# First unit: queries ahead of the keys, more work on VectorE, stacks sent strip by strip, and the test of the square weights at the beginning

## The chip, the cores and the metric

The kernel runs on one core of one Trainium2 chip. The metric is the device time of one execution in microseconds, as the median of three runs. The five engines appear in the profile as PE (TensorE, matmuls; PEld is its loading of weights), DVE (VectorE), ACT (ScalarE), POOL (GpSimd) and SP (SyncE, which here does nothing but issue DMAs). SPq and ACTq are the DMAs that the SP and the ACT queue issue; while ACT issues a DMA it does nothing else.

## The reference

Eight sequences of 512 positions and 128 features go through six attention layers and then through a gated network. The attention is unusual: the softmax weights of 16 heads are averaged, a decay is added, and a second softmax of that sum is applied to `h` itself.

```python
def layer(h, p):
    q = (h @ wq.T + bq_).reshape(bh, sl, H, DH)      # H = 16, DH = 8
    k = (h @ wk.T + bk_).reshape(bh, sl, H, DH)
    scores = jnp.einsum('blhd,bmhd->bhlm', q, k) * inv_sqrt_d
    w_avg = jax.nn.softmax(scores, axis=-1).mean(axis=1)
    new_w = jax.nn.softmax(CSCALE * w_avg + rel[None], axis=-1)
    sa = jnp.einsum('blm,bme->ble', new_w, h)
    h1 = _ln(h + sa, l1w, l1b)
    h2 = _ln(h1, l2w, l2b)
    ff = jax.nn.relu(h2 @ w1.T + b1_) @ w2.T + b2_
    return (_ln(h2 + ff, l3w, l3b), None)

x = x + layers(_layernorm(x))                        # 6 layers, 8 sequences of (512, 128)
h = _layernorm(x)
h = jax.nn.silu((h @ w1.T) * s1) * ((h @ w2.T) * s2) # 128 -> 512
h = gelu((h @ h1.T) * sh1); h = gelu((h @ h2.T) * sh2)  # 512 -> 512, twice
return x + (h @ w3.T) * s3                           # 512 -> 128
```

`w1_w`, `w2_w`, `h1_w` and `h2_w` of the last network hold only -1, 0 and 1.

## The kernel before

**Units and steps.** The work is cut into 48 units, one for each layer and sequence (layer 0 with sequences 0 to 7, then layer 1, and so on). A unit has four blocks `lc` of 128 query positions, a block has four strips (`turn`) of four heads, and a strip is worked in two halves: 32 steps (`PAIRS`) to a unit. A step issues two matmuls of scores (L461, 128 x 512), two maxima of them on DVE (L472, `top`), and two exponentials on ACT (L481, `e`), so a unit has 64 of each. Every second strip the sums of the exponentials are inverted (L490, `r`), POOL makes from them weights `rp` (L492), and PE gathers the heads into one accumulator (L503, `acc`). After four strips ACT takes the second exponential (L511, `w`), PE transposes it, DVE multiplies it by the decay (L521) and PE applies it to `h` (L529).

**An order written by hand.** There is no scheduler. `at(step, place, fn)` files a piece of work under a step and a place in it (P0 to P2 between the matmuls, D0 to D2 between the maxima, A0 to A2 between the exponentials), and the main loop issues it there. So each engine's order is fixed by the program, and an instruction that waits holds up all that follow on its engine. `plan_before` files what a unit needs before its scores, `plan_after` its norms and its feed-forward part, which run in the two units behind. Steps below 0 are the start, before the first scores.

**Stacks.** A matmul of scores takes its keys from `ks` and its queries from `qs`, both laid out by strip. Keys and queries are split into a high part (12 low bits cleared, `hik`, `hiq`, on DVE, L283) and the rest (`lok`, `loq`, on POOL, L284). POOL multiplies the query parts by a mask of heads (L320, into tiles `m0` and `m1`), and DMAs inside the on-chip memory carry the pieces to their strips: 16 of 64 KB for the keys of a unit (`stack_k`, L299) and 16 of 128 KB for each half of its queries (`stack_q`, L336). For the first half of the first unit `stack_first` (L347) does it in 32 of 64 KB, 16 for each of the blocks 0 and 1. There the keys go first (steps 4 and 6 of the start), the queries after (steps 8, 18 and 19), and the ACT queue issues half of the key DMAs and half of those of block 0. The masked queries of block 1 lie in two of the four buffers of the tiles of exponentials (`e`), which thus come free when those DMAs have landed.

**Start.** SP loads two sequences and all weights of layer 0 (L98, L107 to L113), ACT nine small tables (L127). The first two norms run on DVE (statistics) and POOL (the power of -1/2, then subtract, L210, and multiply, L215). PE's clock is the granted clock of the profile.

**Ring and buffers.** The results of matmuls go to seven banks in a ring (`ps_big`), so PE can be some seven tiles ahead of ACT. The pool `proj` has two buffers each for `ks` and `qs`. DMAs are tracked by eight semaphores in turn, so each DMA issued on SP or ACT waits until the one eight before it has landed.

**Test of the square weights.** Whether the last network may use a cheaper exact product depends on the low 12 bits of the eight 128 x 512 blocks of `h1`, `h2` and of `w1`, `w2`. In the units 41 to 45 `load_square` (steps 1 and 16) brings two blocks each to a staging tile and from there to its place, and `low_bits` (steps 7 and 23) clears the high bits on DVE (L159) and takes the maximum (L162). In unit 47 `low_bits_row` and `low_bits_end` reduce this to one number, which after the last unit chooses an arm of the program.

Of the kernel before, what the change touches and what calls it, by code (L numbers as in the profile page):

```python
# [29 lines left out]
def attn_stack_then_ffn(ctx: ExitStack, tc: tile.TileContext, a: dict, out: bass.AP):  # L30
# [69 lines left out]

    for b in range(2):
        x_in[b] = load_x(b, f"in{b}")
    lay = {}

    def load_layer(d):
        qk = wts.tile([P, 2, E], F32, tag="wqk", name=f"wqk_{d}", bufs=2)
        nc.sync.dma_start(qk, a["wqk"][d].rearrange("t e o -> e t o"))  # L107
# [9 lines left out]
        rows = {name: r[:, k, :] for k, name in enumerate(ROWS)}  # L117
        lay[d] = (qk, w1, w2, rows)

    cols = {}  # L120
    for name, shape in (
        ("bq_col", [P, D]), ("bk_col", [P, D]), ("b1_col", [P, D * FC]),
        ("ln2w_col", [P, D]), ("ln2b_col", [P, D]), ("f_w1s_col", [P, HC]),
        ("f_w2s_col", [P, HC]), ("f_h1s_col", [P, HC]), ("f_h2s_col", [P, HC]),
    ):
        cols[name] = wts.tile(shape, F32, tag=name, name=name)
        nc.scalar.dma_start(cols[name], a[name])  # L127
    load_layer(0)

# [15 lines left out]
    staged = {}  # L145

    def load_square(k):

        name, c = ("f_w1t", "f_w2t", "f_h1t", "f_h2t")[k if k < 2 else 2 + (k - 2) // HC], (k - 2) % HC
        t = staged[k] = state.tile([P, HID], F32, tag="x", name=f"square_{k}", bufs=3)  # L150
        nc.sync.dma_start(t, a[name] if k < 2 else a[name][c * P : (c + 1) * P, :])
        nc.sync.dma_start(
            (fw1, fw2)[k] if k < 2 else (fh1, fh2)[(k - 2) // HC][:, c, :], t
        )

    def low_bits(k):

        t = staged.pop(k)
        nc.vector.tensor_scalar(  # L159
            t.bitcast(I32), t.bitcast(I32), ~LOW12, None, ALU.bitwise_and  # L160
        )
        nc.vector.tensor_reduce(low[:, k : k + 1], t.bitcast(I32), AX.X, ALU.max)  # L162

# [20 lines left out]
    class Norm:  # L184
# [57 lines left out]
    class Unit:  # L242
# [18 lines left out]
        def project_k(self):  # L261
            d = self.d
            pk = ring([P, L], f"pk_{self.n}")
            self.kT = work.tile([P, L], F32, tag="kT", name=f"kT_{self.n}", bufs=1)
            nc.tensor.matmul(pk, lay[d][0][:, 1, :], self.hT, start=True, stop=True)  # L265
            return lambda: nc.scalar.activation(  # L266
                self.kT, pk, AF.Identity, bias=cols["bk_col"][:, d : d + 1]
            )

        def project_q(self):  # L270
            d = self.d
            pq = ring([P, L], f"pq_{self.n}")
            self.qT = work.tile([P, L], F32, tag="qT", name=f"qT_{self.n}", bufs=1)
            nc.tensor.matmul(pq, lay[d][0][:, 0, :], self.hT, start=True, stop=True)
# [18 lines left out]
        def stack_k(self):  # L293


            self.ks = proj.tile([P, STRIPS, L], F32, tag="ks", name=f"ks_{self.n}")
            for c in range(4):
                for i in range(STRIPS):
                    (nc.scalar if self.u == 0 and c % 2 else nc.sync).dma_start(  # L299
                        self.ks[32 * c : 32 * c + 32, i, :],  # L300
                        self.kparts[c % 2][32 * i : 32 * i + 32, :],
                    )

        def mask_q(self, two, k, lc):
# [3 lines left out]
            if self.u == 0 and two == 0:  # L308
                pool, tag = (work, f"m{k}") if lc == 0 else (epool, "e")
                self.stacks[key] = pool.tile(  # L310
                    [P, 2, NB, PER_STRIP, QB], F32, tag=tag, name=f"m{k}_first_{lc}",
                    bufs=1 if lc == 0 else None,
                )
            elif lc == 2 * two:
# [25 lines left out]

        def stack_first(self, lc):

            if lc == 0:
                self.stacks[0] = proj.tile([P, STRIPS, 2, NB * P], F32, tag="qs", name="qs_first")
            for i in range(STRIPS):
                for c in range(4):
                    (nc.scalar if c >= 2 and lc == 0 else nc.sync).dma_start(  # L347
                        self.stacks[0][32 * c : 32 * c + 32, i, lc],
                        self.stacks[0, c // 2][32 * i : 32 * i + 32, lc].rearrange(
                            "p n j l -> p (n j l)"  # L350
                        ),
                    )


        def sum_rows(self):

            rows = lay[self.d][3]
            rows["b2s"] = wts.tile([P, E], F32, tag="b2s", name=f"b2s_{self.d}", bufs=2)
            nc.gpsimd.tensor_tensor(rows["b2s"], rows["ln2_b"], rows["b2"], ALU.add)
# [5 lines left out]
        def affine_a(self, k):  # L365
            rows = lay[self.d][3]
            if k == 0:
# [8 lines left out]
        def affine_b(self, k):  # L376
            rows = lay[self.d][3]
            if k == 0:
# [14 lines left out]
        def hidden(self, f):  # L393
            w1 = lay[self.d][1]
            if f == 0:
# [317 lines left out]
    def plan_before(un):  # L713
# [7 lines left out]
        s = t - PAIRS  # L721
        matmuls(s, (2, P2, 2, A1), un.project_k)
        matmuls(s, (6, P0, 7, A1), un.project_q)
        at(s + 4, D1, un.split_k)
        at(s + 8, D2, un.split_q)
        at(s + 6, D2, un.stack_k)
        for k in range(2):
# [3 lines left out]
        if un.b == 0:  # L731
            at(t + 3, D2, un.sum_rows)
        if un.u == 0:
            for lc in range(2):
                for k in range(2):
                    at(s + 18 + lc, D2, lambda k=k, lc=lc: un.mask_q(0, k, lc))
                at(s + 18 + lc, D2, lambda lc=lc: un.stack_first(lc))
            return
# [285 lines left out]
```

## Time and profile before

| what | value |
|---|---|
| median of 3 runs (lowest, highest) | 2611.12 us (2611.08, 2613.16) |
| the profiled execution's own time | 2611.54 us |
| span of its profile | 2609.7 us |
| busy: PE, DVE, ACT, POOL | 97%, 95%, 94%, 70% |
| first matmul of scores, first exponential | 28.53 us, 30.80 us |
| last exponential starts | 2389.2 us |
| DMA: moved, mean rate | 273.75 MB, 105 GB/s |

The three busiest engines are all close to full for the whole run, so no single one can be named from the shares alone. The first and the last tenth of the profile differ from the middle; the last 220 us are the gated network.

A useful clock of this kernel is the start of the first exponential of each unit, which the timeline shows (64 of them to a unit):

| from unit to unit | us for one unit |
|---|---|
| 0 to 1, 1 to 2 | 49.3, 48.8 |
| 2 to 5 | 49.8 to 49.9 |
| 6 to 40 | 48.9 to 49.1 |
| 41 to 45 | 50.3 each |
| 46 | 49.7 |

### The profile page before, as it was taken

How to read it: one execution, taken by the hardware profiler on the slowest of the kernel's cores; microseconds unless marked ns; L12 is line 12 of the kernel's file. 1: busy time of each engine (PE TensorE's matmuls, PEld its weight loads, DVE VectorE, ACT ScalarE, POOL GpSimd, SP SyncE). 2: the span in 40 equal slices, each digit the busy share in tenths (PEclk: the TensorE clock that was granted, in tenths of full speed). 3: DMA queues.
4: the chain of work that ended last, by engine and by line, in shares of the span. 5: the costliest groups of instructions: out<-in, count | busy, mean ns of one | idle time of the engine just before them, and what ended most of it. 6: DMA issues, size and time to landing. Idle time of an engine off the chain costs nothing.

```text
span 2609.7 us, 51735 instructions
## 1 busy us (share of the span) xinstructions
PE 2526.3 (97%) x14944; PEld 1435.9 (55%) x14944; DVE 2482.6 (95%) x5582; ACT 2450.8 (94%) x6798; POOL 1834.0 (70%) x1990
## 2 busy tenths in 40 slices
PE   5999999999999999999999999999999999998999
PEld 2455555555555555555555555555555555555787
DVE  5999999999999999999999999999999999998874
ACT  5999999999999999999999999999999999997443
POOL 4667777677677677677677677677677667775974
PEclk8999999999999999999999999999999999999999
DMA  5554544444444444444444444444444545541000
GB/s 133 116 120 119 116 112 100 114 114 115 114 114 98 114 110 119 114 114 98 114 113 115 114 109 103 114 113 116 114 113 104 138 117 128 132 102 34 9 25 18
DMA packets 135857, 273.75 MB, mean 105 GB/s; under 512 B 39696, under 2 KB 57232, under 8 KB 135568
## 3 DMA queue, kind: packets, MB, share of 16 engines
q1 hardware_dynamic: 133504, 269.31, 44.1%
q8 instruction: 121, 1.98, 0.3%
q10 hardware_dynamic: 2064, 1.08, 0.2%
q14 instruction: 168, 1.38, 0.2%
HBM read 13.86 MB, written 2.10 MB: 6 GB/s over the span
## 4 chain that ended last, share of the span: by engine, by line
PE 46%; ACT 33%; DVE 12%; issue 4%; POOL 3%; DMA 0%; ACTq 0%; SPq 0%; DVEq 0%; POOLq 0%
ACT e L481 28%; PE ps L461 14%; PE acc L503 13%; DVE top L472 9%; PE py L418 4%; PE qh L589 4%; PE po L529 3%; PE pt_w L222 2%; ACT w L511 2%; PE pf L398 1%; PE fo L635 1%; ACT kT L266 1%; PE q L589 1%; ACT g L406 1%; PE pk L265 1%
## 5 line engine op out<-in xcount | busy, mean ns | idle before, releaser
L481 ACT ACTIVATE e<-ps,top 128x512 f32<-128x512 f32 x3072 | 2137.7, 814 | 19.7 <-DMA qs_first<-m_first 9.3
L472 DVE TENSOR_REDUCE top<-ps 128x1 f32<-128x512 f32 x3072 | 1923.2, 677 | 24.5 <-PE ps L461 19.6
L461 PE MATMUL ps<-ks,qs 128*128 128x512 f32 x3040 | 1153.8, 468 | 16.0 <-ACT e L481 14.1
L481 ACT ACTIVATION_READ_ACCUMULATOR e<-ps,top 128x1 f32 x3072 | 1021.1, 332 | 0.0
L461 PEld LDWEIGHTS ps<-ks,qs 128*128 128x128 f32 x3040 | 524.1, 188 | 623.6 <-ACT e L481 322.4
L503 PE MATMUL acc<-e,rp 128*32 128x512 f32 x6144 | 739.1, 599 | 0.0
L503 PEld LDWEIGHTS acc<-e,rp 128*32 128x32 f32 x6144 | 160.3, 109 | 330.5 <-issue 328.8
L492 POOL TENSOR_TENSOR rp<-pick,r 128x256 f32<-128x256 f32 x384 | 237.2, 618 | 122.6 <-DVE r L490 77.6
L320 POOL TENSOR_TENSOR m<-loq,mask 128x512 f32<-128x512 f32 x190 | 241.6, 1283 | 0.0
L320 POOL TENSOR_TENSOR m<-hiq,mask 128x512 f32<-128x512 f32 x190 | 241.5, 1282 | 0.0
L529 PEld LDWEIGHTS po<-h,wT 128*128 128x128 f32 x1536 | 201.1, 191 | 20.5 <-issue 3.6
L529 PE MATMUL po<-h,wT 128*128 128x129 f32 x1536 | 203.5, 275 | 1.0 <-DVE wT L521 1.0
L284 POOL TENSOR_TENSOR loq<-qT,hiq 128x512 f32<-128x512 f32 x48 | 61.5, 1282 | 197.8 <-DVE hiq L283 173.5
L398 PE MATMUL pf<-uT,w 128*128 128x512 f32 x384 | 195.9, 591 | 0.9 <-ACT ht L625 0.9
L418 PEld LDWEIGHTS py<-w,g 128*128 128x128 f32 x1536 | 186.1, 191 | 8.4
L418 PE MATMUL py<-w,g 128*128 128x128 f32 x1536 | 186.8, 275 | 0.0
L222 PE MATMUL pt_w<-ident,w 128*128 128x128 f32 x768 | 120.6, 279 | 21.8 <-ACT e L481 13.3
L511 ACT ACTIVATE w<-acc 128x512 f32<-128x512 f32 x192 | 135.6, 706 | 1.1 <-PE acc L503 1.1
L521 DVE TENSOR_TENSOR wT<-pt_w,decay 128x512 f32<-128x512 f32 x192 | 130.3, 678 | 0.0
L222 PEld LDWEIGHTS pt_w<-ident,w 128*128 128x128 f32 x768 | 87.7, 140 | 74.6 <-ACT e L481 55.4
L206 POOL TENSOR_TENSOR rs_c<-mv_c,eps 128x4 f32<-128x4 f32 x48 | 9.7, 203 | 166.1 <-DVE mv_c L200 166.1
L406 ACT ACTIVATE g<-pf,b_col 128x512 f32<-128x512 f32 x144 | 125.3, 870 | 0.2 <-PE pf L398 0.2
(118 smaller groups left out, 2633.9 us busy)
## 6 DMA issues: line engine op xcount, KB each, us to landing
qs<-m SPq DMA_DIRECT2D x1520, 128.0 KB, 2.3
ks<-hik SPq DMA_DIRECT2D x384, 64.0 KB, 2.0
ks<-lok SPq DMA_DIRECT2D x376, 64.0 KB, 2.0
rows<-in_rows SPq DMA_DIRECT2D x6, 448.0 KB, 4.8
x_in<-in_x SPq DMA_DIRECT2D x8, 256.0 KB, 3.0
fh<-square SPq DMA_DIRECT2D x8, 256.0 KB, 2.3
x_out<-in_x SPq DMA_DIRECT2D x8, 256.0 KB, 2.8
out<-y SPq DMA_DIRECT2D x7, 256.0 KB, 2.4
```

Of the source, the lines that this page charges most:

```text
L222: nc.tensor.transpose(pt[:, c * P : (c + 1) * P], src[:, c, :], ident)
L320: nc.gpsimd.tensor_tensor(m[:, lc - 2 * two], part.unsqueeze(2).to_broadcast([P, NB, PER_STRIP, QB]), mask.unsqueeze(1).to_broadcast([P, N ...
L398: nc.tensor.matmul(pf, w1[:, f * P : (f + 1) * P], self.uT, start=True, stop=True)
L406: nc.scalar.activation(self.g[:, f, :], pf, AF.Relu, bias=cols["b1_col"][:, k : k + 1])
L418: nc.tensor.matmul(self.py[:, k, :], self.g[:, f, c * P : (c + 1) * P], w2[:, f, :], start=(f == 0), stop=(f == FC - 1),)
L461: nc.tensor.matmul(ps[s], qs[:, nb * P : (nb + 1) * P].bitcast(F32R), un.ks[:, i, :].bitcast(F32R), start=True, stop=True,)
L472: nc.vector.tensor_reduce(top[s], ps[s], AX.X, ALU.max, negate=True)
L481: nc.scalar.activation(self.e[:, nb, :], ps[s], AF.Exp, bias=top[s], accum_out=self.zs[:, i % 2, nb : nb + 1],)
L492: nc.gpsimd.tensor_tensor(self.rp.rearrange("p t n l -> p (t n) l"), pick.unsqueeze(1).to_broadcast([P, 2 * NB, QB]), r.rearrange("p t n - ...
L503: nc.tensor.matmul(acc[nb * QB : (nb + 1) * QB, :], self.rp[:, gr.turn % 2, nb, :], gr.e[:, nb, :], start=(gr.turn == 0), stop=(gr.turn == ...
L511: nc.scalar.activation(self.w.rearrange("p c l -> p (c l)"), acc, AF.Exp, scale=1.0 / H)
L529: nc.tensor.matmul(self.po, self.wT[:, c, :], self.unit.h[:, c, 0 : E + 1], start=(c == 0), stop=(c == LC - 1),)
```

## The change

The start and the first unit are put in another order, and the test of the square weights is moved from the units 41 to 47 to the start and the first unit.

- Loads: SP now issues first the first sequence, `wqk` of layer 0 and the tables `bq_col`, `bk_col`, then ten loads of 256 KB of the square weights for the test (`look_at_square`, into the first `ks` and `qs` buffers), then the second sequence and the seven other tables. ACT loads nothing. `w1`, `w2` and `rows` of layer 0 are loaded in unit 0, behind the first stacks.
- First two norms: subtract and multiply are one DVE instruction per 128 x 128 block (`centre_and_scale`) in place of two POOL instructions.
- First unit: the queries are projected and split before the keys, and `lo` is subtracted on DVE. POOL's masks for the blocks 0 and 1 follow at once; those of block 1 lie in a buffer of `g` and no longer in tiles of exponentials.
- `stack_first` sends keys and queries of block 0 strip by strip: for the strips 0 to 2, four DMAs on SP and four on ACT; for strip 3 all eight on SP. Then 16 for block 1 on SP. In all SP issues 36 and ACT 12 of these (32 and 16 before).
- `sum_rows` (POOL, 0.47 us) moves from step 3 to step 12 of unit 0.
- Test: `low_bits` works on two blocks at a time (128 x 1024) in five parts: parts 0, 1 and 2 before the first scores, parts 3 and 4 at the steps 4 and 6 of unit 0; the reduction to one number at its step 8 and at the first step of unit 1. `load_square` in the units 41 to 45 stays, with its DMAs; the ten DVE pairs there and the two instructions in unit 47 are gone.

```diff
+    x_in[0] = load_x(0, "in0")
+    load_qk(0)
+    load_col("bq_col", [P, D])
+    load_col("bk_col", [P, D])
...
-    low = state.tile([P, 2 + 2 * HC], I32, name="low")
+    low = state.tile([P, 1 + HC], I32, name="low")
...
+    def look_at_square():
+        first = proj.tile([P, 2, HID], F32, tag="ks", name="look_first")
+        rest = proj.tile([P, 2 * HC, HID], F32, tag="qs", name="look_rest")
+        for part in range(1 + HC):
+            looked[part] = first if part == 0 else rest[:, 2 * part - 2 : 2 * part, :]
+            for k in range(2):
+                nc.sync.dma_start(looked[part][:, k, :], square_block(2 * part + k)[0])
...
+    def low_bits(part):
+        t = looked.pop(part).bitcast(I32)
+        nc.vector.tensor_scalar(t, t, ~LOW12, None, ALU.bitwise_and)
+        nc.vector.tensor_reduce(low[:, part : part + 1], t, AX.XY, ALU.max)
...
+    look_at_square()
+    x_in[1] = load_x(1, "in1")
+    for name, shape in other_cols:
+        load_col(name, shape)
...
+        def centre_and_scale(self):
+            for c in range(LC):
+                nc.vector.tensor_scalar(
+                    self.dst[:, c, :], self.src[:, c, :], self.mv[:, c, 0:1], self.rs[:, c : c + 1],
+                    ALU.subtract, ALU.mult,
+                )
...
-            nc.gpsimd.tensor_tensor(lo, t, hi, ALU.subtract)
+            (nc.vector if self.u == 0 else nc.gpsimd).tensor_tensor(lo, t, hi, ALU.subtract)
...
-                pool, tag = (work, f"m{k}") if lc == 0 else (epool, "e")
...
+                        self.m_first = work.tile(
+                            [P, 2, 2, NB, PER_STRIP, QB], F32, tag="g", name="m_first", bufs=1
+                        )
...
+        def stack_first(self):
+            self.ks = proj.tile([P, STRIPS, L], F32, tag="ks", name="ks_first")
+            self.stacks[0] = proj.tile([P, STRIPS, 2, NB * P], F32, tag="qs", name="qs_first")
...
+            for i in range(STRIPS):
+                queries(nc.sync, i, 0, 0)
+                keys(nc.sync, i, 0)
+                other = nc.scalar if i < STRIPS - 1 else nc.sync
+                keys(other, i, 1)
+                queries(other, i, 0, 1)
+            for i in range(STRIPS):
+                for k in range(2):
+                    queries(nc.sync, i, 1, k)
...
+        if un.u == 0:
+            matmuls(s, (4, P0, 4, A0), un.project_q)
+            matmuls(s, (4, P1, 5, A0), un.project_k)
+            at(s + 5, D0, un.split_q)
+            for lc in range(2):
+                for k in range(2):
+                    at(s + (5, 6)[lc], D2, lambda k=k, lc=lc: un.mask_q(0, k, lc))
+            at(s + 6, D0, un.split_k)
+            at(s + 6, D2, un.stack_first)
...
-            at(t + 3, D2, un.sum_rows)
+            at(t + (12 if un.u == 0 else 3), D2, un.sum_rows)
...
+    for k, step in enumerate((-30, -30, -26, 4, 6)):
+        at(step, D2, lambda k=k: low_bits(k))
+    at(8, D2, low_bits_row)
+    at(PAIRS, D2, low_bits_end)
...
         at((U - 7 + k // 2) * PAIRS + (1, 16)[k % 2], D2, lambda k=k: load_square(k))
-        at((U - 7 + k // 2) * PAIRS + (7, 23)[k % 2], D2, lambda k=k: low_bits(k))
-    at((U - 1) * PAIRS + 7, D2, low_bits_row)
-    at((U - 1) * PAIRS + 23, D2, low_bits_end)
...
         if un.b == 4 and un.d + 1 < D:
+            load_qk(un.d + 1)
             load_layer(un.d + 1)
+        if u == 0:
+            load_layer(0)
```

More of the change, by code (lines that the diff above doesn't have):

```diff
@@ L99, in load_x, with load_qk @@
         return t
-    for b in range(2):
-        x_in[b] = load_x(b, f"in{b}")
-    lay = {}
+    lay_qk, lay = {}, {}
+    def load_qk(d):
+        lay_qk[d] = wts.tile([P, 2, E], F32, tag="wqk", name=f"wqk_{d}", bufs=2)
+        nc.sync.dma_start(lay_qk[d], a["wqk"][d].rearrange("t e o -> e t o"))
     def load_layer(d):
-        qk = wts.tile([P, 2, E], F32, tag="wqk", name=f"wqk_{d}", bufs=2)
-        nc.sync.dma_start(qk, a["wqk"][d].rearrange("t e o -> e t o"))
         w1 = wts.tile([P, F], F32, tag="w1", name=f"w1_{d}", bufs=2)
@@ L116, in load_layer, with load_col @@
         )
-        rows = {name: r[:, k, :] for k, name in enumerate(ROWS)}
-        lay[d] = (qk, w1, w2, rows)
+        lay[d] = w1, w2, {name: r[:, k, :] for k, name in enumerate(ROWS)}
+    x_in[0] = load_x(0, "in0")
+    load_qk(0)
     cols = {}
[L121 to L125, printed above, removed]
-        cols[name] = wts.tile(shape, F32, tag=name, name=name)
-        nc.scalar.dma_start(cols[name], a[name])
-    load_layer(0)
+    def load_col(name, shape):
+        cols[name] = wts.tile(shape, F32, tag=name, name=name)
+        nc.sync.dma_start(cols[name], a[name])
+    load_col("bq_col", [P, D])
+    load_col("bk_col", [P, D])
+    other_cols = (
+        ("b1_col", [P, D * FC]), ("ln2w_col", [P, D]), ("ln2b_col", [P, D]),
+        ("f_w1s_col", [P, HC]), ("f_w2s_col", [P, HC]), ("f_h1s_col", [P, HC]),
+        ("f_h2s_col", [P, HC]),
+    )
     fw1 = wts.tile([P, HID], F32, name="fw1")
@@ L139, in load_ffn, with square_block @@
         nc.sync.dma_start(fw3s, a["f_w3s"].partition_broadcast(P))
-    low = state.tile([P, 2 + 2 * HC], I32, name="low")
+    low = state.tile([P, 1 + HC], I32, name="low")
     low_row = state.tile([1, P], I32, name="low_row")
     low_any = state.tile([1, 1], I32, name="low_any")
-    staged = {}
-    def load_square(k):
[L149 to L162, printed above, removed]
+    looked = {}
+    def square_block(k):
+        if k < 2:
+            return a[("f_w1t", "f_w2t")[k]], (fw1, fw2)[k]
+        c = (k - 2) % HC
+        name, t = (("f_h1t", fh1), ("f_h2t", fh2))[(k - 2) // HC]
+        return a[name][c * P : (c + 1) * P, :], t[:, c, :]
+    def look_at_square():
[5 more added lines that the diff above has]
+                nc.sync.dma_start(looked[part][:, k, :], square_block(2 * part + k)[0])
+    def load_square(k):
+        src, dst = square_block(k)
+        t = state.tile([P, HID], F32, tag="x", name=f"square_{k}", bufs=3)
+        nc.sync.dma_start(t, src)
+        nc.sync.dma_start(dst, t)
+    def low_bits(part):
+        t = looked.pop(part).bitcast(I32)
+        nc.vector.tensor_scalar(t, t, ~LOW12, None, ALU.bitwise_and)
+        nc.vector.tensor_reduce(low[:, part : part + 1], t, AX.XY, ALU.max)
     def low_bits_row():
@@ L264, in project_k @@
             self.kT = work.tile([P, L], F32, tag="kT", name=f"kT_{self.n}", bufs=1)
-            nc.tensor.matmul(pk, lay[d][0][:, 1, :], self.hT, start=True, stop=True)
+            nc.tensor.matmul(pk, lay_qk[d][:, 1, :], self.hT, start=True, stop=True)
             return lambda: nc.scalar.activation(
@@ L273, in project_q @@
             self.qT = work.tile([P, L], F32, tag="qT", name=f"qT_{self.n}", bufs=1)
-            nc.tensor.matmul(pq, lay[d][0][:, 0, :], self.hT, start=True, stop=True)
+            nc.tensor.matmul(pq, lay_qk[d][:, 0, :], self.hT, start=True, stop=True)
             return lambda: nc.scalar.activation(
@@ L298, in stack_k @@
                 for i in range(STRIPS):
-                    (nc.scalar if self.u == 0 and c % 2 else nc.sync).dma_start(
+                    nc.sync.dma_start(
                         self.ks[32 * c : 32 * c + 32, i, :],
@@ L308, in mask_q @@
             if self.u == 0 and two == 0:
-                pool, tag = (work, f"m{k}") if lc == 0 else (epool, "e")
[L310 to L313, printed above, removed]
+                key = two, k, lc
+                if lc == 0:
+                    self.stacks[key] = work.tile(
+                        [P, 2, NB, PER_STRIP, QB], F32, tag=f"m{k}", name=f"m{k}_first", bufs=1
+                    )
+                else:
+                    if k == 0:
+                        self.m_first = work.tile(
+                            [P, 2, 2, NB, PER_STRIP, QB], F32, tag="g", name="m_first", bufs=1
+                        )
+                    self.stacks[key] = self.m_first[:, k]
             elif lc == 2 * two:
@@ L339, in stack_q, with queries @@
                     )
[L341 to L347, printed above, removed]
+        def stack_first(self):
+            self.ks = proj.tile([P, STRIPS, L], F32, tag="ks", name="ks_first")
+            self.stacks[0] = proj.tile([P, STRIPS, 2, NB * P], F32, tag="qs", name="qs_first")
+            def queries(queue, i, lc, k):
+                for c in (2 * k, 2 * k + 1):
+                    queue.dma_start(
                         self.stacks[0][32 * c : 32 * c + 32, i, lc],
-                        self.stacks[0, c // 2][32 * i : 32 * i + 32, lc].rearrange(
+                        self.stacks[0, k, lc][32 * i : 32 * i + 32, lc].rearrange(
                             "p n j l -> p (n j l)"
@@ L352, in stack_first, with keys @@
                     )
+            def keys(queue, i, k):
+                for c in (k, k + 2):
+                    queue.dma_start(
+                        self.ks[32 * c : 32 * c + 32, i, :], self.kparts[k][32 * i : 32 * i + 32, :]
+                    )
+            for i in range(STRIPS):
[7 more added lines that the diff above has]
+                    queries(nc.sync, i, 1, k)
         def sum_rows(self):
-            rows = lay[self.d][3]
+            rows = lay[self.d][2]
             rows["b2s"] = wts.tile([P, E], F32, tag="b2s", name=f"b2s_{self.d}", bufs=2)
@@ L365, in affine_a @@
         def affine_a(self, k):
-            rows = lay[self.d][3]
+            rows = lay[self.d][2]
             if k == 0:
@@ L376, in affine_b @@
         def affine_b(self, k):
-            rows = lay[self.d][3]
+            rows = lay[self.d][2]
             if k == 0:
@@ L393, in hidden @@
         def hidden(self, f):
-            w1 = lay[self.d][1]
+            w1 = lay[self.d][0]
             if f == 0:
@@ L412, in mlp_out @@
         def mlp_out(self, half):
-            w2 = lay[self.d][2]
+            w2 = lay[self.d][1]
             self.py = ring([P, 2, E], f"py_{self.n}_{half}")
@@ L430, in affine_c @@
         def affine_c(self, k):
-            rows = lay[self.d][3]
+            rows = lay[self.d][2]
             if k == 0:
@@ L694, in norm_steps @@
         at(base + s2, D2, lambda: un.ln.aggregate())
+        if base < 0:
+            at(base + s3, D2, lambda: un.ln.centre_and_scale())
+            return
         at(base + s3, D2, lambda: un.ln.centre())
@@ L721, in plan_before @@
         s = t - PAIRS
[L722 to L726, printed above, removed]
+        if un.u == 0:
[7 more added lines that the diff above has]
+            at(s + 6, D2, un.stack_first)
+        else:
+            matmuls(s, (2, P2, 2, A1), un.project_k)
+            matmuls(s, (6, P0, 7, A1), un.project_q)
+            at(s + 4, D1, un.split_k)
+            at(s + 8, D2, un.split_q)
+            at(s + 6, D2, un.stack_k)
         for k in range(2):
@@ L731, in plan_before @@
         if un.b == 0:
-            at(t + 3, D2, un.sum_rows)
+            at(t + (12 if un.u == 0 else 3), D2, un.sum_rows)
         if un.u == 0:
[L734 to L737, printed above, removed]
             return
```

## The prediction

> **What bounds the kernel now.** I read the page's shares first, then the busy time of each engine unit by unit, then the timeline around the test of the square weights and of the first unit, and last the clock and DMA rates of the first 40 us.
>
> The shares cannot choose between three nearly full engines. The windows of unit 40 and unit 41 (start, end, length, then busy us of PE, PEld, DVE, ACT, POOL, granted clock, DMA share, GB/s) can:
>
> ```profile
> 1992.20:2041.10 48.90, 48.33 (x296) 26.67 (x292) 48.48 (x110) 48.90 (x141) 35.45 (x40) 1.00 0.50 120
> 2041.10:2091.40 50.30, 49.03 (x296) 26.59 (x292) 50.05 (x114) 49.17 (x140) 34.94 (x39) 1.00 0.52 126
> ```
>
> In unit 40, PE, DVE and ACT are each busy over 48.3 of 48.9 us. Unit 41 has four more DVE instructions, 1.57 us more of DVE, and lasts 1.40 us longer: what is added to DVE in a full unit is paid. The instructions are those of the test (times in ns, least, median, most):
>
> ```profile
> L159 DVE TENSOR_SCALAR square<-square x10: 415/417/417, 2051.3 to 2277.8; 128x512 int32<-128x512 int32 x10
> L162 DVE TENSOR_REDUCE low<-square x10: 685/687/689, 2051.7 to 2278.2; 128x1 int32<-128x512 int32 x10
> ```
>
> The timeline of unit 41 shows where the time is lost:
>
> ```profile
> 2051.27 0.42 DVE L159 TENSOR_SCALAR square<-square 128x512 int32<-128x512 int32 x1
> 2051.72 0.69 DVE L162 TENSOR_REDUCE low<-square 128x1 int32<-128x512 int32 x1
> 2052.32 0.68 DVE L472 TENSOR_REDUCE top<-ps 128x1 f32<-128x512 f32 x1
> ...
> 2055.24 0.69 ACT L481 ACTIVATE e<-ps,top 128x512 f32<-128x512 f32 x1 [0.22 <-DVE top L472]
> ```
>
> The next maximum starts 1.05 us after L159 started, and a few exponentials later ACT waits for DVE. I laid the exponentials of unit 41 over those of unit 40: they agree to 0.01 us up to step 8, are 0.55 us late from step 9, and 1.38 us late from step 25. The tests stand at the steps 7 and 23; behind the loads, at the steps 1 and 16, nothing is late.
>
> The first unit is another matter:
>
> ```profile
> 24.51 15.40 SPq L347 DMA_DIRECT2D qs_first<-m_first  x24
> 39.96 0.58 SPq L98 DMA_DIRECT2D x_in<-in_x  x1
> 40.64 10.20 SPq L336 DMA_DIRECT2D qs<-m  x16
> ...
> 54.21 0.50 PE L461 MATMUL ps<-ks,qs 128*128 128x512 f32 x1
> ...
> 57.24 0.85 ACT L481 ACTIVATE e<-ps,top 128x512 f32<-128x512 f32 x1
> ```
>
> SP issues without a pause at 0.64 us a DMA. 54.21 is the first matmul of block 2, the first user of `qs_0_1`, and 57.24 its exponential. The thirteenth of the sixteen `qs` DMAs completes strip 0; it went out at 40.64 + 12 x 0.64 = 48.3 and landed near 51. So SP had some 3 us in hand, and ACT, which then runs without a gap, set the pace.
>
> ```profile
> 3.00:4.00 1.00, 0.00 (x0) 0.00 (x0) 0.57 (x3) 0.97 (x2) 0.00 (x0) 1.00 1.01 285
> 6.00:7.00 1.00, 0.00 (x0) 0.00 (x0) 0.00 (x0) 0.00 (x0) 0.99 (x1) 1.00 1.03 359
> 18.00:19.00 1.00, 0.00 (x0) 0.00 (x0) 0.00 (x0) 0.00 (x0) 0.00 (x0) 0.80 0.92 215
> 38.00:40.00 2.00, 2.00 (x6) 1.06 (x5) 2.00 (x5) 0.92 (x4) 1.06 (x1) 0.73 0.44 107
> ```
>
> Loads from memory run at 285 to 359 GB/s, copies on the chip at some 215. PE's clock falls to half near 18.6 (0.80 in that us), 4.1 us after its last matmul ended (14.51), and is full again near 39.1.
>
> **The change part by part.**
>
> *Test out of the late units.* Five units lose two tests each. Unit to unit they take 50.3 against 48.93 in the units before: 5 x 1.37 = 6.85 us. The bounds are 0 (if the loads, which stay, caused it; the steps above speak against that) and 10 x 1.05 = 10.5 (all of DVE's time). With the tests gone these units' order is that of the units 6 to 40, so I take 6.85. Unit 47 loses 0.15 + 0.26 us of DVE; at the same rate 0.2 (0 to 0.4).
>
> *Test in the first unit.* Parts 3 and 4 are two instructions over 128 x 1024. From L159 and L162 one part costs between 1.1 (as for 512) and 2.2 us (double); I take 1.9. Both lie in the block 0 of unit 0. They are covered by the wait for `qs_0_1` below, some 6 us of ACT; without it up to 3.8 us would come to light. The parts 0 to 2 run while nothing else needs DVE, once their loads have landed. The extra DMA of `low_row` costs SP 0.6 us after the stacks, where it has slack.
>
> *Up to the masks.* The first sequence has landed by 3.43; statistics and the power end at 5.97 as before. Four DVE instructions of 128 x 128 (between 0.17, the 128 x 6 of L720, and 0.43, the 128 x 512 of L283; I take 0.22) replace two of POOL (1.04 each): 6.9 instead of 8.10. Transposes 1.12 give 8.1; `hT` is copied then and not at 10.09, since ACT issues no tables: 8.7. Query matmul 2.08, `qT` 0.69, `hiq` 0.43: 12.0, and POOL's first mask (1.26) 13.2. Keys: matmul 1.91, `kT` 0.69, `hik` 0.43, `lok` on DVE (0.68 by L521 to 0.98 by L578): 14.6.
>
> *Loads ahead of the stacks.* The stacks stand behind 2.62 MB of test loads and the second sequence, on the same queue, and by the eight semaphores the first stack DMA waits for the second sequence to land. Sequence and `wqk`, 0.38 MB from 2.0, are through by 3.7 with the two tables; ten blocks at 0.73 to 0.92 us (359 and 285 GB/s) end near 11.7; the sequence 0.9 more; a landing takes 0.5 to 1.4 after that. So stacks start at 13.8 (13.1 to 15.5), just behind the mask.
>
> *Stacks.* Strip 0: four issues each on two queues, ACT from about 14.9: 17.5, and 2.0 to land: first matmul 19.5 instead of 28.53. ACT finishes its twelve issues near 22.6, first exponential there instead of 30.80. Block 1 no longer waits for tiles of exponentials, and the later strips land before they are due (strip 3 near 28.6). ACT is through blocks 0 and 1 at 22.6 + 32 x 0.663 + 2.7 (`hT`, `kT`, `qT`, `w`) = 46.5.
>
> *What is late next: `qs_0_1`.* SP has 36 issues before it instead of 24, and four loads instead of one: 13.8 + 36 x 0.64 = 36.8; loads (0.58, 0.48, 0.43, 0.50 and their gaps) 2.2: 39.0; the thirteenth 12 x 0.64 later, 46.7; landing 2.7 (median of the sixteen in the first 56 us) plus 1.5 for the 0.96 MB of `w1`, `w2` and `rows` in front of it, 3 us of transfers of which half is hidden while they are issued: 50.9 (49.5 to 53). PE begins block 2 at 50.9 instead of 54.21: 3.3 us gained, out of the 8 at the first exponential.
>
> *The clock.* PE's last work before this wait is the transpose behind `w`, near 43.2, so it stands still for 7.7 us, more than the 4.1 after which the clock fell before. It will restart at half speed. Before, PE was without a gap from 34.11 until the clock rose at 39.1, 5.0 us; with 0 to 5 us at half speed it loses 0 to 2.5, and DVE (busy 11.03 of 11.09 us in block 2) cannot make that up. I take 2.0.
> [...]
>
> *Moved and hidden.* `sum_rows` must wait for `rows`, landing near 44, and stands before the `rp` of block 1, which PE needs only after 50.9. The keys of unit 1 go out after `qs_0_1`, some 1.5 us earlier than before.
>
> *Sum.* 6.85 + 0.2 + 3.3 - 2.0 = 8.35. Span 2609.7 - 8.35 = 2601.3; the profiled run has 1.84 around it (2611.54), 2603.2; the median lies 0.42 below that run: **2602.8 us**. Its own range: start -1.5 to +4, tests 6.3 to 7.3, so 2599.8 to 2606.3.
>
> **The rivals.**
> 1. *The queue is not late.* If `qs_0_1` lands by 44, ACT sets the pace: 57.24 - 47.2 = 10 gained at the start, no half clock, and DVE's 3.8 come to light: 2611.1 - 7.05 - 6.2 = 2597.9. For it: ACT starts 8 us earlier. Against: 53 issues at 0.64 between the masks and strip 0. Chance 0.07.
> 2. *The loads of squares, not the tests, lengthen the units 41 to 45.* They stay; only the start's 1.3 and 0.2 remain: 2609.6. Against: the steps at which the time is lost. Chance 0.05.
> 3. *Slower: the test loads hold the stacks.* Place: SP's first stack DMA, behind the second sequence. Each us past 13.8 costs one; from 13.8 + 8.35 = 22.2 on, the kernel is slower. That needs loads under 155 GB/s. At 105 GB/s, the mean of the whole run, ten blocks take 25 us, stacks start at 31, and the time is 2620. For it: everything is on one queue. Against: memory loads moved 285 and more. Chance 0.03.
>
> **How the numbers follow.** Forecast 0.85, rivals 0.07, 0.05, 0.03. A measurement of this kernel tells about 0.2%, 5.2 us, from no change, so faster means under 2605.9. The forecast lies there 0.94 of the time: 0.80, with rival 1 0.87. Within 0.2%: the rest of the forecast 0.05 and rival 2 with part of 3, 0.10; slower 0.03. Range 2597.8 to 2607: forecast and rival 1.
>
> **What would show it.** Units 41 to 45 at 48.9 us; first matmul near 19.5 and first exponential near 22.6; first matmul of block 2 near 50.9, with PE idle before it and the clock at half for some us behind; first exponential of unit 1 near 79 instead of 80.1. It is wrong if those five units still take 50.3, or if block 2 starts before 47 or after 56.

## The result, and the profile after

| | median, us | ratio to the kernel before (95%) |
|---|---|---|
| kernel before, 11 runs beside the changed one | 2611.19 | |
| changed kernel, 11 runs (2603.51 to 2607.70) | 2605.65 | 0.9977 (0.9969 to 0.9985) |

The changed kernel is 5.5 us faster, where 8.35 were forecast. The profiled execution is one of 2605.65 us, its span 2603.9 (2609.7 before). I laid the starts of the exponentials of the two profiles beside each other:

| first exponential of | before | forecast | after | gained so far |
|---|---|---|---|---|
| unit 0, block 0 | 30.80 | 22.6 | 24.15 | 6.65 |
| block 1 | 46.16 | | 42.26 | 3.90 |
| block 2 | 57.24 | | 58.13 | -0.89 |
| unit 1 | 80.13 | near 79 | 82.12 | -1.99 |
| unit 2 | 128.9 | | 130.9 | -2.0 |
| unit 41 | 2041.1 | | 2043.2 | -2.1 |
| the last exponential of all | 2389.18 | | 2384.42 | 4.76 |

So the start lost 2.1 us, the units from 41 on gave 6.9, and what comes behind the last exponential was 1.1 shorter (219.4 against 220.5 us; in the runs below it lies between 218.7 and 220.9 with the same work in it). That makes 5.9; the two spans, rounded, differ by 5.8.

The windows of the units 41 and 42 of the changed kernel (columns as before: PE, PEld, DVE, ACT, POOL busy us, granted clock, DMA share, GB/s):

```profile
2043.20:2092.40 49.20, 48.58 (x297) 26.70 (x293) 48.79 (x111) 49.10 (x141) 35.26 (x39) 1.00 0.53 129
2092.40:2141.30 48.90, 48.32 (x296) 26.66 (x292) 48.20 (x110) 48.90 (x141) 34.70 (x39) 1.00 0.53 130
```

The units 42 to 45 take 48.92 us instead of 50.3, with 110 instructions on DVE instead of 114, though the loads of the square weights are still there. The start is in these rows of the timeline, PE first and then ACT with the DMAs that it issues (start, length, and in brackets the idle time before and what ended it):

```profile
20.20 2.04 PE L515 MATMUL ps<-ks_first,qs_first 128*128 128x512 f32 x4 [8.26 <-DMA ks_first<-hik]
...
54.96 1.19 PE L515 MATMUL ps<-ks_first,qs 128*128 128x512 f32 x2 [4.69 <-DMA ks<-hik]
56.08 3.45 PE L557 MATMUL acc<-e,rp 128*32 128x512 f32 x16
59.46 0.97 PE L515 MATMUL ps<-ks_first,qs 128*128 128x512 f32 x3
```

```profile
15.63 1.46 ACTq L394 DMA_DIRECT2D ks_first<-lok  x2
...
22.83 1.28 ACTq L385 DMA_DIRECT2D qs_first<-m_first  x2
24.15 0.69 ACT L535 ACTIVATE e<-ps,top 128x512 f32<-128x512 f32 x1 [11.49 <-DMA ks_first<-lok]
...
36.10 0.69 ACT L535 ACTIVATE e<-ps,top 128x512 f32<-128x512 f32 x1 [2.46 <-DVE top L526]
40.35 0.69 ACT L535 ACTIVATE e<-ps,top 128x512 f32<-128x512 f32 x1 [1.46 <-DVE top L526]
58.13 0.69 ACT L535 ACTIVATE e<-ps,top 128x512 f32<-128x512 f32 x1 [4.56 <-PE acc L557]
```

PE and ACT begin 8.3 and 6.7 us sooner, and it is all spent at 54.96: block 2, which began at 54.21 before, now begins 0.75 us later. The row names `ks<-hik` as what ended that wait, but block 2 still uses `ks_first`; what it needs is `qs`, whose thirteenth DMA lands at 54.8. Next, the gather takes 3.45 us instead of 1.92, so the third scores start at 59.46 instead of 57.16. The two parts of the test (the rows at 36.10 and 40.35) hold ACT for 3.9 us in between.

Why `qs_0_1` is late stands in SP's timeline and in the list of SP's waits (us in total, times, longest), of the changed kernel:

```profile
13.67 1.23 SPq L385 DMA_DIRECT2D qs_first<-m_first  x2
...
21.30 1.25 SPq L385 DMA_DIRECT2D qs_first<-m_first  x2
23.93 1.15 SPq L394 DMA_DIRECT2D ks_first<-hik  x2
...
39.46 0.50 SPq L113 DMA_DIRECT2D rows<-in_rows  x1
40.08 12.79 SPq L372 DMA_DIRECT2D qs<-m  x16
```

```profile
SPq L372 <- DMA rows<-in_rows: 2.0, 1, 2.0
...
SPq L394 <- DMA ks_first<-lok: 1.4, 1, 1.4
...
SPq L372 <- DMA w<-in_w2t: 0.6, 1, 0.6
```

The stacks start at 13.67 as forecast, but SP does not issue without a pause: 1.4 us until a key piece of strip 2, which ACT issued at 20.99, has landed, and among the sixteen `qs` DMAs (12.79 us, 10.20 before) 0.6 and 2.0 us until `w2` and `rows` have. By the eight semaphores the seventh `qs` DMA waits for `w2` and the eighth for `rows`. The chain of waits has how long that took:

```profile
39.46 7.42 DMA rows<-in_rows
```

The thirteenth `qs` DMA goes out at 50.37 instead of 46.7. The DMAs have 4.7 us from issue to landing between 40 and 56 us, by their median:

```profile
qs<-m SPq DMA_DIRECT2D x16, 128.0 KB, 4.7
```

### The profile page after: what moved, and what is told of

It reads as the page before. It is cut to its first block, busy times and chain, and to the rows that moved or that the text cites. A ratio compares the mean times of both kernels' runs of the same rounds, so it can differ in the third digit from the quotient of the medians.

```text
span 2603.9 us, 51821 instructions
## 1 busy us (share of the span) xinstructions
PE 2523.6 (97%) x14944; PEld 1436.8 (55%) x14944; DVE 2490.0 (96%) x5582; ACT 2449.8 (94%) x6798; POOL 1829.5 (70%) x1984
## 4 chain that ended last, share of the span: by engine, by line
PE 52%; ACT 31%; DVE 9%; issue 3%; POOL 3%; SPq 1%; DMA 1%; DVEq 0%; POOLq 0%; ACTq 0%
ACT e L535 26%; PE ps L515 16%; PE acc L557 15%; DVE top L526 6%; PE py L472 5%; PE po L583 4%; PE qh L643 4%; PE pt_w L252 2%; ACT w L565 2%; PE pf L452 1%; PE pk L295 1%; PE fo L689 1%; ACT qT L305 1%; ACT kT L296 1%; ACT g L460 1%
## 5 line engine op out<-in xcount | busy, mean ns | idle before, releaser
L515 PE MATMUL ps<-ks,qs 128*128 128x512 f32 x3008 | 1140.6, 469 | 12.9 <-ACT e L535 10.8
L535 ACT ACTIVATION_READ_ACCUMULATOR e<-ps,top 128x1 f32 x3072 | 1043.2, 340 | 0.0
L515 PEld LDWEIGHTS ps<-ks,qs 128*128 128x128 f32 x3008 | 518.7, 189 | 611.2 <-ACT e L535 308.3
```

Source lines behind the costliest of these rows:

```text
L515: nc.tensor.matmul(ps[s], qs[:, nb * P : (nb + 1) * P].bitcast(F32R), un.ks[:, i, :].bitcast(F32R), start=True, stop=True,)
L535: nc.scalar.activation(self.e[:, nb, :], ps[s], AF.Exp, bias=top[s], accum_out=self.zs[:, i % 2, nb : nb + 1],)
```

## The experiments

Each is the changed kernel with one edit, unless said otherwise. "Block 2" and "unit 1" are their first exponentials in the one execution that was profiled, 58.13 and 82.12 in the changed kernel; the medians are over all executions of a run. The first four runs shared one series of the kernel before (2611.66, 23 runs), the next four another (2610.22, 12 runs), the last two a third (2609.60, 9 runs).

| run | median, us | ratio (95%) | block 2 | unit 1 |
|---|---|---|---|---|
| e1, before without the tests | 2604.45 | 0.9970 (0.9959 to 0.9981) | 57.16 | 80.06 |
| e2, test late again | 2612.85 | 1.0003 (0.9994 to 1.0012) | 57.58 | 81.12 |
| e3, layer's loads behind `qs_0_1` | 2600.40 | 0.9959 (0.9946 to 0.9973) | 52.99 | 75.82 |
| e4, parts 3 and 4 at step 2 | 2606.72 | 0.9980 (0.9971 to 0.9989) | 57.76 | 81.34 |
| e5, PE kept busy | 2602.73 | 0.9973 (0.9962 to 0.9983) | 56.03 | 79.36 |
| e6, `rows` alone behind `qs_0_1` | 2600.27 | 0.9961 (0.9948 to 0.9975) | 54.26 | 77.98 |
| e7, `qs_0_1` strip by strip | 2599.05 | 0.9957 (0.9943 to 0.9971) | 53.09 | 75.89 |
| e8, e3 + e4 + e7 | 2599.62 | 0.9959 (0.9945 to 0.9973) | 50.64 | 75.62 |
| e9, e4 + e7, layer's loads at step 24 | 2597.16 | 0.9951 (0.9938 to 0.9965) | 50.98 | 74.31 |
| e10, e9 without e4 | 2598.78 | 0.9962 (0.9948 to 0.9975) | 52.53 | 75.36 |

### e1: the kernel before, without the tests

```diff
-        at((U - 7 + k // 2) * PAIRS + (7, 23)[k % 2], D2, lambda k=k: low_bits(k))
-    at((U - 1) * PAIRS + 7, D2, low_bits_row)
-    at((U - 1) * PAIRS + 23, D2, low_bits_end)
...
+    nc.vector.memset(low_any, 0)
```

> The kernel before with the ten pairs of the test in the units 41 to 45 and its two reductions in unit 47 left out (the number that they give is set to 0; the loads of the squares stay). Theory (the tests cost 1.37 us of DVE in each of five units): units 41 to 45 take 48.9 us each, unit 1 starts at 80.1 as before, the time is 2611.2 - 7 = 2604.2 us. Rival (the loads of the squares lengthen these units): they still take 50.3 us, the time is about 2611.

Measured: 7.2 us less than the kernel before, with its start as it was and the loads in the units 41 to 45 left in. Its unit 41, in the windows:

```profile
2042.40:2091.30 48.90, 48.32 (x296) 26.70 (x292) 48.49 (x110) 48.90 (x140) 34.95 (x39) 1.00 0.54 130
```

It follows that the tests and not the loads made those units longer, which ends rival 2. Without any of the change's work on the start this kernel is as fast as the changed one (the intervals overlap).

### e2: the changed kernel with the test in the late units again

```diff
-    look_at_square()
...
-    for k, step in enumerate((-30, -30, -26, 4, 6)):
-        at(step, D2, lambda k=k: low_bits(k))
-    at(8, D2, low_bits_row)
-    at(PAIRS, D2, low_bits_end)
...
+        at((U - 7 + k // 2) * PAIRS + (7, 23)[k % 2], D2, lambda k=k: low_bits(k))
+    at((U - 1) * PAIRS + 7, D2, low_bits_row)
+    at((U - 1) * PAIRS + 23, D2, low_bits_end)
```

> The changed kernel with the test put back into the units 41 to 47 as before; its ten loads at the start are gone. Theory (the new start loses because the stack qs_0_1 of the first unit is late in SP's queue, whatever the test does): unit 1 still starts near 82 us (80.1 before, 82.1 changed), units 41 to 45 take 50.3 us, 2613 us. Rivals (the parts of the test in block 0 on DVE, or the test loads ahead of the stacks, make the start slow): unit 1 at 78 or earlier, 2609 us.

Measured: the gain is gone (the interval holds 1), and the units 41 to 45 take 50.3 us again. Block 1 starts at 37.45 instead of 42.26, since neither the ten early loads nor the parts 3 and 4 are in the way, and yet the first matmul of block 2 is at 54.40 and unit 1 at 81.12:

```profile
54.40 1.19 PE L514 MATMUL ps<-ks_first,qs 128*128 128x512 f32 x2 [7.77 <-DMA qs<-m]
```

So half of the start's loss of 2.0 us stays without the test (unit 1 was at 80.13 in the kernel before), and unit 1 is still 2.1 us behind the forecast 79: what holds block 2 is not upstream on DVE or ACT, it is the `qs` DMA.

### e3: the loads of the layer behind `qs_0_1`

```diff
         if u == 0:
-            load_layer(0)
+            at(5, D2, lambda: load_layer(0))
...
-            at(t + (12 if un.u == 0 else 3), D2, un.sum_rows)
+            at(t + (28 if un.u == 0 else 3), D2, un.sum_rows)
```

> The changed kernel with the loads of w1, w2 and rows of layer 0 behind the stack qs_0_1 (step 5 of unit 0; sum_rows at its step 28). Theory (these loads and the wait for rows to land hold up qs_0_1 by 4 to 6 us): first matmul of block 2 at 48 to 50 us instead of 54.96, PE's clock stays full there, unit 1 starts at 76 to 77.5, the time is 2600 us. Rival (parts 3 and 4 of the test on DVE set the start): unit 1 at 81 to 82, 2605 us.

Measured: 0.9959 against the changed kernel's 0.9977, 4.7 us of 2611; in the profiles unit 1 starts 6.3 us sooner. The two intervals touch, but the slowest execution of e3 (2602.32) is faster than the fastest of the changed kernel (2603.51). Its PE timeline:

```profile
49.88 0.49 PE L515 MATMUL ps<-ks_first,qs 128*128 128x512 f32 x1
...
50.98 1.92 PE L557 MATMUL acc<-e,rp 128*32 128x512 f32 x16
```

The scores of block 2 follow block 1's transpose without a wait (no bracket in the row), and the gather takes 1.92. With three DMAs taken from ahead of `qs_0_1` on SP, the whole of the start's loss is gone, and with it the slow gather (3.45 us in the changed kernel, at a clock of 0.50 until 59.2). (`sum_rows` moved too; e7 leaves it where it was.)

### e6: only `rows` behind `qs_0_1`

e3 moves three DMAs and their bytes. Two readings were left: that the eighth issue waits for `rows` to land, or that SP's time and the bytes of all three matter.

```diff
         if u == 0:
             load_layer(0)
+            at(5, D2, lambda: load_rows(0))
...
-            at(t + (12 if un.u == 0 else 3), D2, un.sum_rows)
+            at(t + (28 if un.u == 0 else 3), D2, un.sum_rows)
```

(`load_rows` is the last part of `load_layer`, left out of it for layer 0.)

> The changed kernel with the load of rows alone (448 KB) behind qs_0_1, sum_rows at step 28; w1 and w2 stay ahead. Theory A (SP's wait for rows to land, 2.0 us by a semaphore, is the main part of the 4 to 5 us): first matmul of block 2 at 51 or earlier, unit 1 at 77 to 78, 2601.5 us. Theory B (every byte ahead counts alike; rows are 448 of 960 KB): first matmul near 52.5, unit 1 near 79, 2603 us.

Measured: the time is e3's (2600.27 and 2600.40). SP's and PE's timelines:

```profile
38.97 10.49 SPq L378 DMA_DIRECT2D qs<-m  x16
49.51 0.58 SPq L119 DMA_DIRECT2D rows<-in_rows  x1
```

```profile
51.22 1.07 PE L521 MATMUL ps<-ks_first,qs 128*128 128x512 f32 x2 [1.78 <-DMA qs<-m]
52.21 3.17 PE L563 MATMUL acc<-e,rp 128*32 128x512 f32 x16
```

The sixteen issues take 10.49 us again, and block 2's first matmul comes at 51.22, 3.7 us sooner than in the changed kernel and within 0.3 of the 50.9 that I had forecast for the changed kernel itself. Of the 3.7 us, SP's earlier arrival at `qs_0_1` makes 1.1 (38.97 against 40.08; 0.6 is the issue of `rows` itself, the other 0.5 a difference between the two profiles ahead of that place), the waits inside the sixteen issues 2.3 (10.49 against 12.79), and the landing the rest, 0.3. So one DMA of 448 KB, mainly through the landing that the eighth one behind it must wait for, is the term that was missing; the wait for `w2` goes with it. The gather is still slow here (3.17 us), and unit 1 gains 4.1.

### e7: `qs_0_1` strip by strip

Block 2 needs the four DMAs of strip 0. In the change's order they are the first, fifth, ninth and thirteenth; here they are the first four, and `rows` stays where it was.

```diff
-            for c in (2 * k, 2 * k + 1):
-                for i in range(STRIPS):
...
+            parts = [(c, i, m) for c in (2 * k, 2 * k + 1) for i in range(STRIPS)]
+            if self.u == 0:
+                self.later = parts if k == 0 else sorted(self.later + parts, key=lambda p: (p[1], p[0]))
+                parts = self.later if k else []
+            for c, i, src in parts:
```

> The changed kernel with the sixteen DMAs of qs_0_1 issued strip by strip, so that strip 0 is complete with the fourth and not with the thirteenth; all loads stay ahead. Theory (only the place of strip 0 in SP's queue makes block 2 late): first matmul of block 2 by 49, block 2 on ACT right behind block 1 (53.4 instead of 58.1), unit 1 at 76 to 77.5, 2600.5 us. Rival (the transfers ahead of it saturate the DMA engines, so any order lands as late): unit 1 at 80 or later, 2604 us or more.

Measured: 2599.05 us. SP waits as long as ever, and nobody needs what it is late with:

```profile
39.58 13.55 SPq L375 DMA_DIRECT2D qs<-m  x16
```

```profile
49.30 0.66 PE L252 MATMUL pt_w<-ident,w 128*128 128x128 f32 x4 [0.66 <-ACT w L568]
49.97 0.50 PE L518 MATMUL ps<-ks_first,qs 128*128 128x512 f32 x1
...
51.06 1.92 PE L560 MATMUL acc<-e,rp 128*32 128x512 f32 x16
```

### e4: the parts 3 and 4 of the test at step 2

```diff
-    for k, step in enumerate((-30, -30, -26, 4, 6)):
+    for k, step in enumerate((-30, -30, -26, 2, 2)):
```

> The changed kernel with parts 3 and 4 of the test at step 2 of unit 0, where DVE waits for PE, and not at the steps 4 and 6. Theory (their 3.9 us on ACT are covered by the wait for qs_0_1): block 1 starts 3 to 4 us earlier (42.3 in the changed kernel), block 2 and unit 1 as late as there (82), 2605.6 us. Rival (they set the start): unit 1 at 78.2, 2601.8 us.

Measured: block 1 starts 4.0 us sooner (38.24), and unit 1 only 0.8; the ratio (0.9980) is the changed kernel's. PE waits for `qs<-m` instead:

```profile
54.59 1.19 PE L515 MATMUL ps<-ks_first,qs 128*128 128x512 f32 x2 [7.72 <-DMA qs<-m]
```

The 3.9 us of DVE are covered by that wait, as the prediction had it.

### e5: PE kept at work in front of block 2

Twelve matmuls on old data, whose result nobody uses, stand between block 1's transpose and block 2.

```diff
+        for _ in range(12):
+            nc.tensor.matmul(
+                t, un.stacks[0][:, 0, 0, 0:P].bitcast(F32R), un.ks[:, 0, :].bitcast(F32R),
+                start=True, stop=True,
+            )
```

> The changed kernel with twelve more matmuls of scores (0.33 us each, 4 us in all, their result is not used) on PE just before block 2 of unit 0, where PE waits for qs_0_1 from 50.3 to 55.0. Theory (the wait halves PE's clock, and the half clock behind it costs 1.5 us): the clock is full from 55 on or soon after, the gather behind the first two matmuls of block 2 takes 1.9 us instead of 3.45, unit 1 starts at 80.5 to 81 instead of 82.1, 2604 us. Rival (PE's pace does not matter there): unit 1 at 82, 2605.6 us.

Measured, in the windows of the changed kernel first and then of this one (the clock is the third column from the right):

```profile
52.00:54.00 2.00, 0.00 (x0) 0.00 (x0) 0.00 (x0) 1.57 (x6) 0.00 (x0) 0.59 0.99 203
54.00:56.00 2.00, 1.04 (x2) 0.50 (x2) 0.24 (x1) 0.00 (x0) 0.00 (x0) 0.50 0.58 142
56.00:58.00 2.00, 2.00 (x13) 0.60 (x16) 1.76 (x4) 0.00 (x0) 0.07 (x1) 0.50 0.46 113
```

```profile
50.00:54.00 4.00, 2.85 (x12) 2.03 (x12) 1.48 (x4) 3.14 (x10) 0.00 (x0) 1.00 0.86 198
54.00:58.00 4.00, 3.78 (x26) 1.87 (x27) 2.75 (x6) 1.48 (x5) 1.11 (x2) 1.00 0.58 136
```

The twelve matmuls take 3.00 us (0.25 each, where 0.33 were expected). The clock stays at 1.00, the gather takes 1.92 us, and from block 2's first matmul (54.22) to its first exponential it takes 1.81 instead of 3.17: the half clock costs 1.4 us there, and unit 1 comes 2.76 sooner, of which 0.74 is the earlier landing. The ratio only moves from 0.9977 to 0.9973, with overlapping intervals: what the profile shows is too small for the medians.

### e8: the three edits together

The edits are those of e3, e4 and e7.

> The changed kernel with the loads of layer 0 behind qs_0_1, parts 3 and 4 of the test at step 2, and qs_0_1 strip by strip. Theory (with the wait gone, the 3.9 us of the test in block 0 come to light and are saved too): block 1 at 38.2, block 2 at 49.5, unit 1 at 72 to 73.5, 2597 us. Rival (something else holds unit 1 at the 75.8 of the run with the loads behind): 2600 us.

Measured: block 2 at 50.64, the earliest of all runs, but unit 1 at 75.62, no better than e3 or e7 alone, and 2599.62 us. The gain is lost between block 3 and unit 1, in PE's and SP's timelines:

```profile
73.14 0.70 PE L518 MATMUL ps<-ks,qs 128*128 128x512 f32 x2 [2.00 <-ACT e L538]
73.77 3.46 PE L560 MATMUL acc<-e,rp 128*32 128x512 f32 x16
```

```profile
50.08 0.50 SPq L113 DMA_DIRECT2D rows<-in_rows  x1
50.69 2.43 SPq L329 DMA_DIRECT2D ks<-hik  x4
53.22 3.48 SPq L329 DMA_DIRECT2D ks<-lok  x4
...
62.52 10.13 SPq L375 DMA_DIRECT2D qs<-m  x16
```

The row gives an exponential as what ended PE's wait. I read the 2.0 us otherwise, as the same wait one unit on: SP issues from `qs_0_1` to unit 1's own queries without a gap, the loads that were moved behind `qs_0_1` and a wait for `rows` (in the 3.48) stand ahead of `qs_1_0`, and its thirteenth DMA goes out at 70.1 and lands 2.9 us later, at 73.0, just before PE begins. e9 was made to test that.

### e9: the loads at step 24

```diff
-            at(5, D2, lambda: load_layer(0))
+            at(24, D2, lambda: load_layer(0))
...
-            at(t + (28 if un.u == 0 else 3), D2, un.sum_rows)
+            at(t + (35 if un.u == 0 else 3), D2, un.sum_rows)
```

(beside e8, of which the other edits stay)

> The changed kernel with three edits: qs_0_1 issued strip by strip (as in e7), parts 3 and 4 of the test at step 2 (as in e4), and load_layer(0) later than in e3: at step 24, with sum_rows at step 35, so that the queue has qs_0_1, ks_1 and qs_1_0 ahead of it without the wait for the landing of rows. Theory (in e8 unit 1 waited for qs_1_0, whose issues stood behind the loads and the wait for rows): qs_1_0 is issued some 3 us sooner than in e8, PE does not wait for it, unit 1's first exponential comes at 72.5 to 73.5 against 75.62, and the time is 2596.5 to 2597.5. Rival (something else, the clock or the engines, holds unit 1): its first exponential stays near 75.6 and the time near 2599.5.

Measured: 2597.16 us, in the forecast stretch; the queries of unit 1 go out 2.6 us sooner than in e8 (59.93), PE does not wait for them, and that reading of e8 holds (in place of the 2.00, no wait). But unit 1 is at 74.31, 0.8 past the forecast. (The profiled execution took 2600.56 us, the other four 2596.05 to 2597.64, so the profile shows more loss than the median.) Between blocks 1 and 2 12.8 us pass instead of the 11.1 of e10. Most of these 1.7 us is one more wait for a landing, in the timelines of DVE and ACT:

```profile
41.13 0.49 DVE L216 BATCH_NORM_STATS2 st_in<-x_in 128x6 f32<-128x128 f32 x2 [1.40 <-DMA x_in<-in_x]
```

```profile
42.30 0.69 ACT L538 ACTIVATE e<-ps,top 128x512 f32<-128x512 f32 x1 [1.29 <-DVE top L529]
```

With the test out of the way, DVE comes to the statistics of the third sequence before that has landed (SP issues it at 37.05, just ahead of `qs_0_1`, and it takes 4.0 us), and the maxima behind them are late. From one exponential to the next that makes 2.13 us instead of 0.66, 1.5 of the 1.7. In e8 DVE waits 1.30 us at the same place, in e2 1.14 and in e4 0.59; in e10 it comes there at 42.90 and does not wait. The rest, 0.24 us before block 2 and another 0.63 in it, goes with a fall of the clock at the beginning of block 2, with PE at work:

```profile
46.60:50.00 3.40, 3.04 (x14) 1.43 (x18) 3.40 (x8) 3.40 (x11) 0.00 (x0) 0.59 0.80 182
```

### e10: the parts 3 and 4 back, the rest as in e9

> e9 with parts 3 and 4 of the test back at steps 4 and 6, where the change has them. In the changed kernel they held ScalarE 2.46 and 1.46 us in block 0, and block 2 waited for qs_0_1 anyway. Theory (they are free only under that wait): with qs_0_1 no longer late they come to light, unit 1's first exponential comes 3 to 4 us later than in e9 (near 76), and the time is 3 to 4 us over e9's. Rival (covered by another wait): within 1 us of e9 in unit 1 and in the time.

Measured: between the two. Block 1 is 3.3 us later than in e9 (41.47), with the same two waits of 2.44 and 1.46 us of ACT for DVE; no DMA covers them any more, as the first matmul of block 2 (49.48) follows the transpose directly. Yet unit 1 is only 1.05 later, because e9 lost 1.5 us of its lead to the wait for the third sequence and 0.9 to the clock, and e10 did not (its clock is 1.00 from 42 to 62 us). The medians differ by 1.6 us, and the two intervals overlap. So the price of the uncovered parts is some 3.3 us where they stand, of which nearly half is covered by that other wait; that 1 to 2 us are left at the end, the intervals do not show.

## Why the prediction was right, and where not

*Test out of the late units: right.* 6.85 + 0.2 were forecast and the late units gave 6.9; e1, with nothing else changed, 7.2. Rival 2 (the loads) is out.

*Loads ahead of the stacks, masks, first strips: right.* Forecast 13.8 for the stacks, 13.67 measured; first matmul 19.5 and 20.20; first exponential 22.6 and 24.15, late because ACT began its twelve issues at 15.63 instead of 14.9 and took 8.5 us for them (to 24.11) instead of 7.7. Rival 3, which needed stacks 8 us later, never came near.

*Parts 3 and 4: right.* 3.8 forecast, 3.92 measured (2.46 + 1.46), and covered by the wait for `qs_0_1`, as e4 shows. That they come to light without it is right in kind (e10); at the end they cost less than 3.8, since DVE without them waits for the third sequence (e9).

*What is late next: right in kind, wrong in size.* The prediction named `qs_0_1` as what ends the start, and that holds. The term that was mis-sized is "12 x 0.64 later, 46.7" and the landing at 50.9 behind it: it was 54.96, and the start's +1.3 (3.3 - 2.0) became -2.0. The 4.0 us are SP 1.1 later when it reaches `qs_0_1` (40.08 against 39.0: the pause of 1.4 for a key piece, in part made good), 2.6 of waits among the first twelve issues, and 0.4 more in landing. The text knew the eight semaphores and used them for the first stack DMA; it did not use them for the four loads which the change puts directly ahead of `qs_0_1`. In the trace of before nothing stood in that place but the load of a sequence, so its 0.64 us to an issue was a rate without such waits. e6 takes `rows` from ahead of the stack and finds 51.22.

*The clock: right.* 2.0 forecast, 1.4 to 2.0 by e5. PE's last work before the wait ended at 50.27, and the clock fell at 52.4, 2.1 us later (4.1 us in the kernel before). It was at half until 59.2, and of that PE was at work from 54.96, 4.2 us, within the 0 to 5 of the forecast.

*Rival 1 (the queue is not late, 2597.9 us)* is what e3, e7, e9 and e10 make of the change: 2597.16 to 2600.40. e3 and e7 do no less work than the changed kernel: the order of one queue (and, in e3, the step of `sum_rows`) decides between the two cases. The rival's own sum was too large, however: with the parts 3 and 4 paid it had 6.2 us gained at block 2, and e3, e7 and e10 gained 4.2 to 4.7 (52.53 to 53.09 against 57.24). e9 is the fastest that was run, 0.9951 (0.9938 to 0.9965) of the kernel before; that it is faster than e7 or e10 the intervals do not show.

*The total: in part luck.* The start came out at -2.1 us (at unit 41), below the -1.5 that the prediction gave as its worst case. The tests were as forecast, and the 1.1 us behind the last exponential, which no term of the sum contains and which vary by 2.2 us between profiles with the same work, made good a part.

## What to carry to other kernels

When DMAs are tracked by a few semaphores in turn, write down for each late and large load which issue waits for its landing (here the eighth behind it), and put nothing urgent there; a small issue time says nothing of it (`rows` took 0.50 us to issue and 7.42 to land). Within a group of DMAs, issue first what the first user needs: e7 kept all of SP's waits and lost none of the time. And of an earlier start count only what reaches the next place at which all engines meet: 6.7 us at the first exponential were nothing two blocks later. The order of a queue also sets what comes to light next: with the stack in time and the test out of block 0, DVE waited for the next load (e9).

## What the runs showed of the hardware that was not expected

*The clock also falls while PE works.* In the second half of unit 1 PE waits for DVE and ACT in places. In e1 and e8 the clock halves for 3.4 us right behind such a stretch, in which PE was busy 2.2 of 3.4 us; the kernel before goes through the same stretch with PE as busy and keeps its clock. Windows of e1, of e8 and of the kernel before:

```profile
111.00:114.40 3.40, 2.23 (x9) 0.98 (x7) 3.40 (x8) 3.40 (x10) 2.05 (x3) 1.00 0.91 205
114.40:117.80 3.40, 3.40 (x17) 0.59 (x16) 2.67 (x9) 3.40 (x11) 2.45 (x4) 0.50 0.90 204
```

```profile
108.20:111.60 3.40, 2.24 (x12) 1.09 (x15) 3.40 (x8) 3.40 (x12) 1.84 (x2) 0.99 0.91 205
111.60:115.00 3.40, 3.40 (x16) 0.50 (x15) 2.44 (x9) 3.40 (x11) 2.68 (x4) 0.50 0.92 209
```

```profile
110.80:114.20 3.40, 2.23 (x10) 0.94 (x8) 3.40 (x7) 3.37 (x10) 2.31 (x3) 1.00 0.84 190
114.20:117.60 3.40, 3.40 (x24) 1.60 (x25) 3.40 (x11) 3.40 (x11) 2.19 (x3) 1.00 0.90 204
```

Unit 1 takes 48.8 us in the kernel before and 50.4 in e1, whose instructions there are the same. PE's busy time does not tell the two apart in these rows (2.23 of 3.40 us in both, and 3.40 of 3.40 behind). What decides was not shown. In the ten runs' profiles unit 1 takes 48.7 to 51.9 us, and the ones above 50 (e1, e2, e4, e8, e9) all show such a stretch at half clock: from 84 to 124 us their granted clock is 0.96 on the mean, as it is in e10, and 1.00 in the others. So a difference of 1.5 us between two profiles of this kernel can come from one such stretch alone.

*And it stays low while PE works.* In the changed kernel it is at 0.50 until 31.9 although PE begins at 20.20, busy for 1.80 us up to 22, then for 1.50, 0.79 and 0.53 in each 2; from 28.60 to 32.00 PE was busy all the time. In the kernel before it stayed at 0.50 while PE was busy for 2.86 of 3.42 us (32.25 to 35.67), until 39.1. What brings it back was not shown.

*One load of 448 KB took 7.4 us to land*, while the 16 DMA engines were 97% busy (236 GB/s from 39.5 to 46.9 us); the median of the six such loads of the run is 4.8.
